# Sorting single columns of 104 edges with 128 places instead of double columns of 232 with 256, in a scatter-add kernel

## The chip, the cores and the metric

One core of a Trainium2 chip runs the whole program in one launch. The metric is the device time of one execution in microseconds (us); smaller is better. The engines are TensorE (PE; its weight loads are PEld), VectorE (DVE), ScalarE (ACT), GpSimd (POOL) and SyncE (SP, which here only issues transfers).

## The reference

There are 6250 nodes of 128 features and 206,250 edges of 128 features, fp32. The features of the edges are summed by the node in `src`; then a small network and a layer norm run over the nodes.

```python
x, src, dst, edge_attr_128          # (6250, 128), (206250,), (206250,), (206250, 128)
edge_aggr = jnp.zeros((n, 128)).at[src].add(edge_attr_128)
global_expand = jnp.repeat(global_feat, n, axis=0)
combined = jnp.concatenate([x, edge_aggr, global_expand], axis=-1) @ W_c + b_c
h = jax.nn.softplus(combined @ W1 + b1)
h = jax.nn.softplus(h @ W2 + b2)
out = layernorm(x + (h @ W3 + b3))
```

`src` is in no useful order. `dst` is not used by the result.

## The kernel before

**The sum over edges.** The nodes are cut into `NB` = 25 blocks of `BL` = 256. The kernel brings the edges of one block together in DRAM and then sums them with TensorE: 128 sorted edges (a chunk) are the stationary operand, and a one-hot block of 128 x 256, which says for each edge which of the 256 nodes it belongs to, is the moving one. The product is added into `sums_t`, which holds the sums of all nodes, features on partitions.

**Groups.** `GROUPS` cuts the edges into ten groups, given as (pairs, columns, sub). A group's edges are scattered into one of `PLACES` = 3 DRAM buffers (`place0` to `place2`), and while the next group is scattered, it is read back in chunks and reduced. A run of `sub` x 128 rows of a buffer holds edges of one block alone; rows that no edge fills keep what `fill_rows` wrote, or rows of an older group, whose node codes differ by `code_of(g)` and match nothing.

**Two ways into the buffer.** A plain column is 128 edges, one to a partition, that one indirect transfer writes row by row (516 bytes each: 128 features and the node code) to positions from `pos_of`. A pair is first sorted on chip. It is 232 edges, 120 on the partitions of one half and 112 of the other (`PA`, `PB`), which are put into 256 places by block so that each block's run begins at an even place. Two neighbouring places then go out as one run of 1032 bytes, so one indirect transfer of 128 runs takes the place of two of 128 rows.

**The sort.** `sort_steps(i)` handles one piece of five pairs. For each pair, `compare` makes the one-hot blocks `sort_hot` on ScalarE (two Abs of 256 columns, one Relu of 512), `gather` multiplies them with the edges on TensorE (four fp32 matmuls of 129 columns, two for each half of the places), and `settle` copies the result out of PSUM on ScalarE. The three are run for the next piece, within the loop's turn before its scatter.

**Positions.** `positions(g)` makes the list of steps that work out where each edge of a group goes. For pairs, the steps `count_set`, `count_set2`, `count_set3`, `place_set`, `rank_set` and `rank_set2` work on sets of `STEP` = 20 pairs, with pairs and blocks along the free dimension (500 elements), the same on all partitions. For plain columns they are `count`, `count2`, `scan`, `place` and `place2`; `totals` and `chunk_map` give the group's layout.

**The order.** TensorE, VectorE, ScalarE and SyncE run in the order in which the program issues their work. The main loop goes over groups and, in each, over pieces (ten plain columns or five pairs, mixed evenly). At each piece it loads the piece `LEAD` = 4 ahead, copies node codes in (`code_rows`), scatters the piece at hand, and then runs a share of four lists, merged evenly: the positions of the next group, the reduction of the last one (`reduce_steps`), the node rows, and the fill of the next group's buffer. `AHEAD` says by which part of the group a list is done.

**The reduction.** `reduce_steps(g)` reads `CHUNK_ROWS` = 1024 rows at a time (`load`), makes one-hot blocks of four chunks each (`match`: one VectorE instruction, or four Abs and a Relu on ScalarE), multiplies (`product`) and adds the result of each run of `sub` chunks to `sums_t` (`add`). `TAIL` says for the last four groups how loads are shared between VectorE and ScalarE: with (100, 2, 5, 5) a load i of these groups goes to ScalarE unless i modulo the number is its highest remainder.

```python
GROUPS = ((0, 40, 1), (40, 40, 2), (80, 80, 4), (100, 110, 4), (100, 110, 4), (100, 110, 4),
          (60, 80, 4), (40, 40, 2), (0, 40, 1), (0, 20, 1))
```

After the last group the node network runs over 13 tiles of up to 512 nodes.

## Time and profile before

| | |
|---|---|
| median of 3 runs | 2342.2 us (2340.88 to 2345.74) |
| the profiled execution | 2346.94 us; its span, first to last instruction, 2345.2 us |
| busy: TensorE, its weight loads | 1878.4 us (80%), 1547.6 us (66%) |
| busy: VectorE, ScalarE, GpSimd | 1424.1 us (61%), 1371.8 us (58%), 1227.8 us (52%) |
| transfers | 471.68 MB, mean 201 GB/s |
| mean granted TensorE clock | 0.914 |

A row of a group reads: line, engine, operation, output and inputs, shapes and count; then busy time in us and the mean of one in ns; then the idle time of the engine just before these instructions, and what ended it. Mean times overlap where an engine starts an instruction before the last has ended; busy time counts each moment once. A row of a stretch of time reads: from and to, length, then for each engine its busy time and the number of instructions, the granted clock, the share of the 16 DMA engines, and what they moved. A row of transfers reads: what, who issues it, count, KB each, and the median time from issue to landing.

### The profile page before, as it was taken

How to read it: one execution, taken by the hardware profiler on the slowest of the kernel's cores; microseconds unless marked ns; L12 is line 12 of the kernel's file. 1: busy time of each engine (PE TensorE's matmuls, PEld its weight loads, DVE VectorE, ACT ScalarE, POOL GpSimd, SP SyncE). 2: the span in 40 equal slices, each digit the busy share in tenths (PEclk: the TensorE clock that was granted, in tenths of full speed). 3: DMA queues.
4: the chain of work that ended last, by engine and by line, in shares of the span. 5: the costliest groups of instructions: out<-in, count | busy, mean ns of one | idle time of the engine just before them, and what ended most of it. 6: DMA issues, size and time to landing. Idle time of an engine off the chain costs nothing.

```text
span 2345.2 us, 31352 instructions
## 1 busy us (share of the span) xinstructions
PE 1878.4 (80%) x9590; PEld 1547.6 (66%) x9590; DVE 1424.1 (61%) x2493; ACT 1371.8 (58%) x3024; POOL 1227.8 (52%) x1258
## 2 busy tenths in 40 slices
PE   2567668888899788999779888879998667767886
PEld 0446556777778677778567777769888555646753
DVE  8687558648785578875368768447775011115767
ACT  0535445765555565555355454454444899986976
POOL 4664655776666566556456545565546123362006
PEclk9878779989999999999889999989999799898998
DMA  9999899979989698778477766768776444345442
GB/s 274 282 293 284 230 282 269 265 199 278 262 234 257 168 251 226 192 208 216 125 208 190 180 173 179 186 187 227 204 216 171 134 113 133 115 129 163 131 141 73
DMA packets 433910, 471.68 MB, mean 201 GB/s; under 512 B 35788, under 2 KB 305060, under 8 KB 433742
## 3 DMA queue, kind: packets, MB, share of 16 engines
q1 hardware_dynamic: 387133, 359.77, 59.4%
q0 software_dynamic: 46464, 109.88, 14.8%
q8 instruction: 77, 1.26, 0.2%
q14 instruction: 92, 0.75, 0.1%
q10 hardware_dynamic: 144, 0.02, 0.0%
HBM read 272.49 MB, written 200.11 MB: 202 GB/s over the span
## 4 chain that ended last, share of the span: by engine, by line
PE 44%; DMA 19%; ACT 16%; DVE 6%; issue 6%; POOL 5%; SPq 3%; DVEq 0%; ACTq 0%; POOLq 0%
PE part L599 30%; PE sorted L789 11%; DMA place<-fill 6%; ACT hot L580 6%; DMA chunks<-place 4%; POOL place L826 4%; DMA place<-rows,pos 3%; ACT hot L582 3%; DMA rows<-in_edge_attr 3%; SPq L158 3%; ACT sort_hot L779 2%; ACT sort_hot L781 2%; POOL place L820 1%; DVE hot L585 1%; DMA place<-pairs,pair 1%
## 5 line engine op out<-in xcount | busy, mean ns | idle before, releaser
L599 PE MATMUL part<-hot,chunks 128*128 128x256 f32 x4726 | 1181.2, 407 | 259.7 <-DVE hot L585 135.7
L599 PEld LDWEIGHTS part<-hot,chunks 128*128 128x128 f32 x4726 | 943.8, 205 | 452.2 <-ACT hot L582 151.4
L820 POOL DMA_INDIRECT place<-pairs,pair x520 | 520.9, 1002 | 621.6 <-ACT pairs L793 466.9
L826 POOL DMA_INDIRECT place<-rows,pos x669 | 653.8, 977 | 361.2 <-issue 217.0
L585 DVE SCALAR_TENSOR_TENSOR hot<-chunks,iota_ps 128x1024 f32<-128x1024 f32 x472 | 558.9, 1214 | 206.0 <-DMA chunks<-place 125.6
L793 ACT COPY pairs<-sorted 128x258 f32<-128x258 f32 x520 | 188.0, 368 | 823.2 <-PE sorted L789 796.1
L789 PE MATMUL sorted<-rows,sort_hot 120*128 120x129 f32 (+1 forms) x4160 | 562.8, 289 | 104.4 <-ACT sort_hot L781 93.9
L789 PEld LDWEIGHTS sorted<-rows,sort_hot 120*128 120x128 f32 (+1 forms) x4160 | 540.4, 201 | 143.0 <-ACT sort_hot L781 110.4
L619 DVE TENSOR_TENSOR sums_t<-sums_t,part 128x256 f32 x803 | 335.9, 418 | 329.9 <-PE part L599 302.2
L779 ACT ACTIVATE sort_hot<-by_slot,slot 120x256 f32<-120x256 f32 x1040 | 467.9, 498 | 5.2 <-DVE slot L388 5.2
L781 ACT ACTIVATE sort_hot<-sort_hot,ones 120x512 f32<-120x512 f32 x520 | 375.3, 722 | 16.9
L580 ACT ACTIVATE hot<-iota_f,chunks 128x256 f32<-128x256 f32 x475 | 201.0, 494 | 37.9 <-DMA chunks<-place 24.8
L582 ACT ACTIVATE hot<-hot,ones 128x1024 f32<-128x1024 f32 (+1 forms) x119 | 136.4, 1146 | 3.9
L1043 POOL TENSOR_TENSOR x_sb<-x_sb,b_all 128x512 f32<-128x512 f32 (+1 forms) x13 | 15.3, 1212 | 114.5 <-PE y_ps L985 114.3
L757 ACT COPY rows<-pair_i 120x5 f32<-120x5 f32 x208 | 30.8, 199 | 42.1 <-DMA place<-rows,pos 21.0
L388 DVE TENSOR_REDUCE slot<-small 128x20 f32<-128x500 f32 x52 | 34.8, 673 | 32.9 <-PE small L384 32.9
L694 DVE COPY x_t<-small 128x512 f32<-128x512 f32 (+1 forms) x13 | 8.6, 659 | 60.5 <-PE small L692 60.5
L489 DVE TENSOR_TENSOR first<-small,ib 128x500 f32<-128x500 f32 (+2 forms) x35 | 22.8, 651 | 30.5 <-PE small L480 30.1
L352 DVE TENSOR_TENSOR set_start<-first,even 128x500 bf16<-128x500 f32 x26 | 17.7, 683 | 37.5 <-PE small L382 36.3
L491 DVE TENSOR_REDUCE pos<-first 128x20 int32<-128x500 f32 (+2 forms) x35 | 37.5, 1070 | 1.2
L500 DVE COPY end_t<-small 25x1 f32<-25x1 f32 x10 | 1.4, 144 | 59.6 <-PE small L499 59.6
L457 DVE TENSOR_TENSOR_SCAN so_far<-iota_ps,ib 128x1500 bf16<-128x1500 f32 (+4 forms) x15 | 37.0, 2469 | 0.0
(164 smaller groups left out, 869.3 us busy)
## 6 DMA issues: line engine op xcount, KB each, us to landing
chunks<-place SPq DMA_DIRECT2D x295, 516.0 KB, 4.9
place<-fill SPq DMA_DIRECT2D x306, 258.0 KB, 9.5
rows<-in_edge_attr SPq DMA_DIRECT2D x66, 640.0 KB, 8.9
rows<-in_edge_attr SPq DMA_DIRECT2D x104, 300.0 KB, 6.4
rows<-in_edge_attr SPq DMA_DIRECT2D x104, 280.0 KB, 7.5
place<-rows,pos POOLq DMA_INDIRECT x669, 6.4
place<-pairs,pair POOLq DMA_INDIRECT x520, 5.7
x_sb<-in_x SPq DMA_DIRECT2D x24, 256.0 KB, 5.4
```

The lines of the kernel that those rows point to most:

```text
L158: ins = engine.dma_start(out, in_).ins
L580: nc.scalar.activation(hot[:, j], codes, AF.Abs, bias=chunks[i][:, lo + j, D:W], scale=-1.0)
L582: nc.scalar.activation(hot[:, :m], hot[:, :m], AF.Relu, bias=ones[:, :1], scale=-1.0)
L585: nc.vector.scalar_tensor_tensor(hot[:, :m], chunks[i][:, lo:lo + m, D:W].to_broadcast([P, m, BL]), code_of(g), iota_ps.unsqueeze(1).to_br ...
L599: nc.tensor.matmul(part[:, s - q, :], t[:, s * sub + j, :D], hot_of[i, (s * sub + j) // HALF * HALF][:, (s * sub + j) % HALF], start=(j == ...
L619: nc.vector.tensor_add(here, here, part[:, s - q, :])
L779: nc.scalar.activation(hot[:PA, q], by_slot.rearrange("p a b -> p (a b)")[:PA], AF.Abs, bias=slot[:PA, q, t0 + j:t0 + j + 1], scale=-1.0)
L781: nc.scalar.activation(hot[:PA], hot[:PA], AF.Relu, bias=ones[:PA, :1], scale=-1.0)
L789: nc.tensor.matmul(out[:, half, :], hot[:n, q, half * P:(half + 1) * P], two[:n, q * PAIRS + j, :], start=(q == 0), stop=(q == 1))
L793: nc.scalar.copy(sets_at[i][:, j], sums_of.pop(j))
L820: s = nc.gpsimd.indirect_dma_start(out=dst, out_offset=bass.IndirectOffsetOnAxis(ap=at, axis=0), in_=rows[:, j].rearrange("p a b -> p (a b ...
L826: s = nc.gpsimd.indirect_dma_start(out=dst, out_offset=bass.IndirectOffsetOnAxis(ap=at, axis=0), in_=rows[:r, j, :], in_offset=None)
```

## The change

The pair now has two single columns of 104 edges (`PN`), and each column is sorted by itself into 128 places, of which 64 runs of two go out; the two columns share one indirect transfer of 128 runs. A piece is six plain columns or three pairs (`LOAD_COLS` = 6). There are 600 pairs instead of 520 and 637 plain columns instead of 669, in eight groups that all have `sub` = 2, and two places.

- Sort: a unit is up to three columns of one parity. `compare` makes three Abs of 128 columns and one Relu on ScalarE, `gather` three fp32 matmuls of 129 columns with 104 rows, `settle` two copies of 64 partitions. `sort_steps(i)` settles the piece two ahead of the one being scattered, gathers the one three ahead and compares the one four ahead (`COMPARED` = 4). Loads run `LEAD` = 8 pieces ahead, node codes `CODED` = 5.
- Positions of pairs: four columns and their 26 buckets stand on 104 partitions (`KB`), so that counts, running sums and jumps of a set of 20 columns are matmuls with tables of 104 x 104 and VectorE operations of a few elements. The places within a column no longer depend on the group's totals.
- `TAIL` gives one load in three of the last four groups to ScalarE.

The diff, cut to what carries it; "..." marks what is left out.

```diff
-GROUPS = ((0, 40, 1), (40, 40, 2), (80, 80, 4), (100, 110, 4), (100, 110, 4), (100, 110, 4),
-          (60, 80, 4), (40, 40, 2), (0, 40, 1), (0, 20, 1))
-LOAD_COLS = 10
-PA, PB = 120, 112
+GROUPS = ((0, 60, 2), (70, 50, 2), (90, 50, 2), (130, 60, 2), (140, 90, 2), (170, 80, 2),
+          (0, 160, 2), (0, 70, 2))
+LOAD_COLS = 6
+PN = 104
 STEP = 20
+QUAD = 4
+THREE = 3
-TAIL = (100, 2, 5, 5)
+TAIL = ((1, 3), (1, 3), (1, 3), (1, 3))
-PLACES = 3
+PLACES = 2
-LEAD = 4
+LEAD = 8
+CODED = 5
+COMPARED = 4
...
-        sets_p = phase.enter_context(tc.tile_pool(name="sets", bufs=4))
+        sets_p = phase.enter_context(tc.tile_pool(name="sets", bufs=5))
-        sort_p = phase.enter_context(tc.tile_pool(name="sort", bufs=4))
+        sort_p = phase.enter_context(tc.tile_pool(name="sort", bufs=5))
...
             def count_set(t):
+                ib = pairs_in.tile([PN, STEP, NB + 1], BF16, name="pair_ib")
                 in_set[t] = ib
+                cols = slice(2 * s0 + t, 2 * s0 + t + STEP)
                 nc.vector.tensor_tensor(
+                    ib, pair_block[:, cols].unsqueeze(2).to_broadcast([PN, STEP, NB + 1]),
+                    iota_ps[:PN, :NB + 1].unsqueeze(1).to_broadcast([PN, STEP, NB + 1]),
                     op=ALU.is_equal)
...
+                small = whole(ps.tile([P, 4, P], F32, name="small", bufs=2))
+                small_of[t] = small
+                for q in range(per_set):
+                    nc.tensor.matmul(
+                        small[:KB, 500 + q:501 + q],
+                        ib[:, q * QUAD:(q + 1) * QUAD].rearrange("p t b -> p (t b)"),
+                        ones_h[:PN, :1], start=True, stop=True)
+
+            def even_set(t):
+                q0 = t // QUAD
+                even_i = per.tile([KB, per_set], I32, name="even_i")
+                small = small_of[t]
+                nc.vector.tensor_scalar(even_i, small[:KB, 500:500 + per_set], 1.0, None,
+                                        op0=ALU.add)
+                nc.vector.tensor_scalar(even_i, even_i, 510, None, op0=ALU.bitwise_and)
+                nc.vector.tensor_copy(evens[:, q0:q0 + per_set], even_i)
+                nc.tensor.matmul(small[:KB, 506:506 + per_set], lower_h,
+                                 evens[:, q0:q0 + per_set], start=True, stop=True)
+
+            def rank_set(t):
+                q0 = t // QUAD
+                small = small_of[t]
+                nc.vector.tensor_copy(starts[:, q0:q0 + per_set], small[:KB, 506:506 + per_set])
+                spread = pairs_in.tile([KB, per_set, P], BF16, name="spread")[:, :, :KB]
+                nc.vector.tensor_tensor(
+                    spread, unit_h.unsqueeze(1).to_broadcast([KB, per_set, KB]),
+                    starts[:, q0:q0 + per_set].unsqueeze(2).to_broadcast([KB, per_set, KB]),
+                    op=ALU.mult)
+                pr = small[:PN, :STEP * NB]
+                nc.tensor.matmul(pr, rank_h, in_set.pop(t)[:, :, :NB], start=True, stop=False)
+                for q in range(per_set):
+                    nc.tensor.matmul(
+                        pr[:, q * QUAD * NB:(q + 1) * QUAD * NB], ones_h[:KB, :PN],
+                        spread[:, q].rearrange("k (t b) -> k t b", b=NB + 1)[:, :, :NB],
+                        start=False, stop=(q == per_set - 1))
+
+            def slot_set(t):
+                nc.vector.tensor_reduce(
+                    slot_of[g][:PN, t:t + STEP],
+                    small_of.pop(t)[:PN, :STEP * NB].rearrange("p (t b) -> p t b", b=NB),
+                    axis=mybir.AxisListType.X, op=ALU.max)
...
+            def pair_set(t):
+                q0 = t // QUAD
+                past = pairs_in.tile([KB, per_set, P], BF16, name="spread")
+                nc.vector.tensor_tensor(
+                    past, twice[:KB].unsqueeze(1).to_broadcast([KB, per_set, P]),
+                    starts[:, q0:q0 + per_set].unsqueeze(2).to_broadcast([KB, per_set, P]),
+                    op=ALU.is_ge)
+                small = whole(ps.tile([P, 4, P], F32, name="small", bufs=2))
+                small_of["pair", t] = small
+                for q in range(per_set):
+                    for h in range(2):
+                        nc.tensor.matmul(small[:, q * QUAD:(q + 1) * QUAD], past[:, q],
+                                         got["jump"][:, q0 + q, h], start=(h == 0), stop=(h == 1))
+
+            def pair_set2(t):
+                at = small_of.pop(("pair", t))[:, :STEP].rearrange("p (b two) -> p b two", two=2)
+                for n in range(2):
+                    rows = slice(64 * n, 64 * n + 64)
+                    nc.vector.tensor_scalar(pair_of[g][rows, t // 2:(t + STEP) // 2],
+                                            at[rows, :, n], half_p[rows], None, op0=ALU.add)
...
-            for n, t in enumerate(sets):
+            for t in sets:
+                if t:
+                    steps.append(lambda t=t: rank_set(t - STEP))
                 steps.append(lambda t=t: count_set(t))
-                steps.append(lambda t=t: count_set2(t))
-                if n:
-                    steps.append(lambda t=t: count_set3(t - STEP))
+                if t:
+                    steps.append(lambda t=t: slot_set(t - STEP))
+                steps.append(lambda t=t: even_set(t))
...
-                share = TAIL[g - G] if g >= G - len(TAIL) else 1
-                if i % share != share - 1:
+                by, of = TAIL[g - G] if g >= G - len(TAIL) else (0, 1)
+                if i % of < by:
...
-                for q, (e, n) in enumerate(((0, PA), (PA * TB, PB))):
-                    rows_dma(two[:n, q * PAIRS:q * PAIRS + k, :D],
-                             edge_attr[e:e + n * TB, :].rearrange("(p t) d -> p t d",
-                                                                  p=n)[:, c:c + k, :])
+                rows_dma(two[:PN, :2 * k, :D],
+                         edge_attr[:E0, :].rearrange("(p t) d -> p t d",
+                                                     p=PN)[:, 2 * c:2 * (c + k), :])
...
+        def compare(unit):
+            i, lo, m, n = unit
+            g, _, c, _, _ = pieces[i]
             slot = slot_of[g]
+            hot = sort_p.tile([P, THREE, P], F32, name="sort_hot")
+            hot_of[unit] = hot
+            for j in range(m):
+                at = 2 * (c - groups[g][4] + lo + j) + n
+                nc.scalar.activation(hot[:PN, j], by_slot[:PN], AF.Abs,
+                                     bias=slot[:PN, at:at + 1], scale=-1.0)
+            nc.scalar.activation(hot[:PN, :m], hot[:PN, :m], AF.Relu, bias=ones[:PN, :1],
+                                 scale=-1.0)
+
+        def gather(unit):
+            i, lo, m, n = unit
+            hot = hot_of.pop(unit)
+            out = ps.tile([P, THREE, W], F32, name="sorted", bufs=2)
+            sorted_of[unit] = out
+            for j in range(m):
+                nc.tensor.matmul(out[:, j, :], hot[:PN, j],
+                                 rows_at[i][:PN, 2 * (lo + j) + n, :], start=True, stop=True)
+
+        def settle(unit):
+            i, lo, m, n = unit
+            if i not in sets_at:
+                sets_at[i] = sets_p.tile([P, PAIRS, 2, W], F32, name="pairs")
+            out = sorted_of.pop(unit)
+            for h in range(2):
+                nc.scalar.copy(sets_at[i][64 * n:64 * n + 64, lo:lo + m, h, :],
+                               out[64 * h:64 * h + 64, :m, :])
+
+        def sort_steps(i):
+            first, second, third = (units(i + COMPARED - k) for k in range(3))
             steps = []
+            for u in range(max(len(first), len(second), len(third))):
+                def one(u=u):
+                    if u < len(third):
+                        settle(third[u])
+                    if u < len(second):
+                        gather(second[u])
+                    if u < len(first):
+                        compare(first[u])
                 steps.append(one)
             return steps
...
                     load_rows(i + LEAD)
-                    code_rows(i + LEAD - 1, True)
+                    code_rows(i + CODED, True)
                     code_rows(i, False)
                     scatter_rows(i)
+                    now = [sort_steps(i)]
                     i += 1
...
-                    now.append(sort_steps(i))
```

Left out are the steps `all_sets` to `goals3`, run once a group, which turn the counts of all sets into the group's totals and into the jump from each bucket's place to its position, the function `tables`, which makes the constant tables once on VectorE, and the sizes of tiles that follow from the new shapes.

More of the change, by code (lines that the diff above doesn't have):

```diff
@@ L221, in whole_nodes @@
         def whole_nodes(part, n):
[L222 to L225 removed]
+            node = scratch("first")[:part.shape[0], :n]
+            wrap = scratch("second")[:part.shape[0], :n]
             nc.vector.tensor_copy(node, part)
@@ new lines, in all_sets3, with goals @@
+            def all_sets3():
+                got["all"] = per.tile([P, NB], F32, name="all")
+                nc.vector.tensor_copy(got["all"], small_of.pop("all")[:, 256:256 + NB])
+            def goals():
+                small = whole(ps.tile([P, 4, P], F32, name="small", bufs=2))
+                small_of["goals"] = small
+                goal = per.tile([1, QUAD, NB + 1], F32, name="goal")
+                nc.vector.tensor_copy(goal[:, :, :NB],
+                                      got["next"][:1].unsqueeze(1).to_broadcast([1, QUAD, NB]))
+                nc.vector.memset(goal[:, :, NB:], FAR)
+                nc.tensor.matmul(small[:KB, :1], goal.rearrange("p t b -> p (t b)"),
+                                 ones[:1, :1], start=True, stop=True)
@@ new lines, in goals2 @@
+            def goals2():
+                small = small_of["goals"]
+                base = per.tile([KB, 1], F32, name="base")
+                nc.vector.tensor_copy(base, small[:KB, :1])
+                nc.vector.scalar_tensor_tensor(
+                    earlier[:, :quads], earlier[:, :quads], base, starts[:, :quads],
+                    op0=ALU.add, op1=ALU.subtract)
+                nc.tensor.matmul(small[:KB, 128:128 + quads], minus, earlier[:, :quads],
+                                 start=True, stop=True)
@@ L519, in positions @@
                 if k == 0 and sets:
-                    steps.append(lambda: count_set3(sets[-1]))
+                    steps.append(all_sets3)
                 if k:
@@ L761, in code_rows, with units @@
             copy(rows_at[i][:r, :k, D:W], low[:r, c:c + k].unsqueeze(2))
[L763 removed]
+        def units(i):
             if i >= len(pieces) or pieces[i][1] != "pair":
                 return []
[L767 to L803 removed]
@@ L858 @@
             node_codes(0)
-            for i in range(LEAD - 1):
+            for i in range(CODED):
                 code_rows(i, True)
```

302 lines of the change are left out of this document (142 added, 160 removed).

## The prediction

> **What bounds the kernel now.** I cut the span where GpSimd's count of scatters (the x of POOL) reaches the end of each group (40, 80, 160, 210, 210, 210, 140, 80, 40, 19) and read the busy times stage by stage; the page's shares mix stages with different limits.
>
> ```profile
> core 0: us, PE busy (x) PEld busy (x) DVE busy (x) ACT busy (x) POOL busy (x), PEclk, DMA share, GB/s
> 0.00:30.10 30.10, 5.55 (x13) 1.29 (x13) 23.67 (x74) 1.79 (x5) 6.83 (x9) 1.00 0.92 268
> 30.10:90.90 60.80, 30.57 (x119) 16.68 (x119) 52.88 (x106) 21.30 (x54) 41.01 (x41) 0.96 1.04 276
> 90.90:234.10 143.20, 97.15 (x461) 74.46 (x461) 101.39 (x196) 66.64 (x159) 81.27 (x81) 0.78 1.07 289
> 234.10:483.30 249.20, 191.62 (x1004) 157.41 (x1004) 161.23 (x272) 141.08 (x331) 159.57 (x160) 0.85 0.94 258
> 812.40:1169.80 357.40, 309.08 (x1702) 263.93 (x1702) 245.72 (x366) 190.61 (x451) 207.33 (x211) 0.95 0.75 203
> 1169.80:1545.80 376.00, 323.01 (x1720) 274.30 (x1719) 255.64 (x407) 190.81 (x451) 207.39 (x210) 0.92 0.70 183
> 1545.80:1789.70 243.90, 232.62 (x1284) 207.99 (x1283) 168.82 (x237) 115.38 (x271) 136.17 (x141) 0.98 0.79 215
> 1789.70:2035.40 245.70, 172.64 (x776) 138.71 (x774) 36.02 (x93) 214.86 (x427) 78.56 (x86) 0.87 0.44 123
> 2035.40:2104.20 68.80, 46.61 (x213) 35.86 (x211) 9.00 (x23) 64.76 (x124) 39.32 (x44) 0.95 0.46 135
> ```
>
> Three regimes: until 483 us the DMA engines are full (share 0.92 to 1.07, about 280 GB/s). From 812 to 1790 us TensorE sets the pace, busy 0.865 of the first of these stages (309.08 of 357.40 us), 0.859 of the second, 0.954 of the third. From 1790 us it is ScalarE (0.874, then 0.94), with VectorE busy for 36 of 246 us: TAIL gives ScalarE all one-hot blocks of group 6.
>
> Next, the groups of the stage from 812.4 to 1169.8 us, for prices and for what TensorE waits on.
>
> ```profile
> L599 PE MATMUL part<-hot,chunks 128*128 128x256 f32 x810 | 194.7, 396 | 18.2 <-DVE hot L585 18.2
> L789 PE MATMUL sorted<-rows,sort_hot 112*128 112x129 f32 (+1 forms) x790 | 103.9, 283 | 20.6 <-ACT sort_hot L781 18.9 <-ACT pairs L793 1.7
> L585 DVE SCALAR_TENSOR_TENSOR hot<-chunks,iota_ps 128x1024 f32<-128x1024 f32 x102 | 120.7, 1214 | 30.9 <-PE part L599 16.4 <-DMA chunks<-place 14.4
> ```
>
> An fp32 matmul is two records. A chunk (128 sorted edges) costs 2 x 194.7/810 = 0.48 us, a sort record 103.9/790 = 0.1315 us. Of the 48 us in which TensorE is idle, 18.2 wait for VectorE and 18.9 for ScalarE's sort blocks.
>
> **The new work.** Chunks follow from the code's formula: two times (rows + 25 x 255) // 256, where a group's rows are 128 x columns + 256 x pairs. For the eight groups that is 108, 238, 278, 368, 418, 468, 208 and 136, together 2222 (2363 before). Stage n scatters group n, reduces group n-1, prepares group n+1. There are 600 + 637 scatters (520 + 669 before).
>
> **TensorE, sort.** A pair falls from eight records to four: 0.526 us instead of 1.052. Over all: 2400 x 0.1315 = 316 us against 4160 x 0.1315 = 547.
>
> **TensorE, positions.** A set of 20 columns (60 sets, each of 10 pairs, replace 26 of 20 pairs) now issues one matmul of 500 columns and 21 short ones, of 1, 4, 5 or 100 columns, each with its own weight load. No short bf16 matmul stands in the trace. The nearest rows:
>
> ```profile
> L379 PE MATMUL small<-pair_ib,before_h 128*128 128x500 bf16 x52 | 21.1, 406 | 10.9 <-DVE slot L388 10.9
> L379 PEld LDWEIGHTS <-before_h 128*128 128x128 bf16 x52 | 5.3, 102 | 0.7 <-issue 0.3
> L658 PE MATMUL small<-cols,wc_sb 128*128 128x1 f32 x2 | 0.3, 209 | 0.0
> L475 PE MATMUL small<-ib,upto_h 128*128 128x500 bf16 (+2 forms) x35 | 14.1, 403 | 0.0
> L692 PE MATMUL small<-ident,x_sb 128*128 128x128 f32 (+1 forms) x49 | 8.7, 304 | 16.7 <-DMA x_sb<-in_x 16.6
> L700 PE MATMUL small<-x_t,fold 128*128 128x512 f32 (+1 forms) x26 | 13.6, 608 | 0.0
> ```
>
> From below, the load alone: 0.10 us. From above, load and the whole record of a one-column matmul, 0.102 + 0.209 = 0.31. I take 0.13, near the lower end, since records overlap (the sort's mean is 283 ns, its share 131). A set is 21 x 0.13 + 0.41 = 3.1, with something for the 100 columns 3.2 us (2.5 to 6.9). Row positions stay: five passes of 0.40 us for 20 columns. So do the node rows, 22.3 us over three stages.
>
> **ScalarE.** A unit of three columns costs three Abs of 128, a Relu of 384 and two copies of 387 elements.
>
> ```profile
> L779 ACT ACTIVATE sort_hot<-by_slot,slot 120x256 f32<-120x256 f32 x1040 | 467.9, 498 | 5.2 <-DVE slot L388 5.2
> L781 ACT ACTIVATE sort_hot<-sort_hot,ones 120x512 f32<-120x512 f32 x520 | 375.3, 722 | 16.9
> L582 ACT ACTIVATE hot<-hot,ones 128x1024 f32<-128x1024 f32 (+1 forms) x119 | 136.4, 1146 | 3.9
> L580 ACT ACTIVATE hot<-iota_f,chunks 128x256 f32<-128x256 f32 x475 | 201.0, 494 | 37.9 <-DMA chunks<-place 24.8
> L793 ACT COPY pairs<-sorted 128x258 f32<-128x258 f32 x520 | 188.0, 368 | 823.2 <-PE sorted L789 796.1
> ```
>
> From 512 to 1024 columns the time rises by 424 ns, 0.83 ns a column. So an Abs of 128 lasts 498 - 106 = 392 ns. Two in a row overlap by 96 (467.9/1040 = 450 against 498), which leaves 392 + 2 x 296 = 984 for three. The Relu takes 722 - 106 = 616, a copy 368 + 107 = 475, and copies that overlap as the Abs do 430. A unit is 2.46 us (2.74 with no overlap at all), so a pair costs 1.64 us, and before 450 x 2 + 722 + 368 = 1.99, for more edges. Per edge that is a draw. TAIL's new (1, 3) for the last four groups gives every third load of eight chunks to ScalarE: 8 x 0.423 + 2 x 1.146 = 5.68 us.
>
> [...]
>
> **VectorE.** Per load of eight chunks: two matches and four additions, 2 x 1.214 + 4 x 0.418 = 4.1 us (two additions before in the groups of sub 4).
>
> ```profile
> L619 DVE TENSOR_TENSOR sums_t<-sums_t,part 128x256 f32 x803 | 335.9, 418 | 329.9 <-PE part L599 302.2
> L388 DVE TENSOR_REDUCE slot<-small 128x20 f32<-128x500 f32 x52 | 34.8, 673 | 32.9 <-PE small L384 32.9
> L369 DVE SCALAR_TENSOR_TENSOR first<-set_start,two_p,first 128x520 f32<-128x520 bf16 x26 | 19.7, 759 | 0.9
> L341 DVE TENSOR_TENSOR all<-all,all_more 128x25 f32<-128x25 f32 x19 | 3.5, 186 | 0.7
> L360 DVE TENSOR_TENSOR_SCAN second<-by_block,first 128x500 f32<-128x500 f32 x26 | 31.2, 1199 | 0.9
> ```
>
> A set has four operations of 500 to 640 elements (about 0.7 to 0.8 us by L388 and L369) and six of a few elements (0.19 by L341): 4.1 us. Stage 4: 46 loads x 4.1 + 17 sets x 4.1 + some 25 for rows and nodes = 283 us, below TensorE's 321: no bound. What goes is place_set, a step with a dozen operations up to 1.2 us long (L360) in a row; TensorE's 18.2 us of waiting for hot blocks stands behind such steps. What comes is a short exchange between TensorE and VectorE at each step of a set, with TensorE's own matmul queued behind VectorE's answer. The sort blocks, made four pieces ahead, no longer make TensorE wait (18.9). I let these cancel and keep the share 0.865.
>
> **DMA.** Fills go from 306 to 222 (80.8 to 58.5 MB) as two places replace three.
>
> ```profile
> chunks<-place SPq DMA_DIRECT2D x295, 516.0 KB, 4.9
> place<-fill SPq DMA_DIRECT2D x306, 258.0 KB, 9.5
> place<-rows,pos POOLq DMA_INDIRECT x669, 6.4
> L826 POOL DMA_INDIRECT place<-rows,pos x669 | 653.8, 977 | 361.2 <-issue 217.0 <-DMA rows<-in_edge_attr 68.9 <-DMA cols<-in_L_gnn_b 22.6
> L619 DVE TENSOR_TENSOR sums_t<-sums_t,part x803: 399/420/443, 106.1 to 2269.2; 128x256 f32 x161
> ```
>
> The first scatter waits until SyncE's queue has passed group 0's fill: 7.1 MB of it, eight loads (3.1) and the indices (0.8) are 11.1 MB, at 268 GB/s 41 us (30 before). Queued behind on SyncE, the later loads start later by the same. With two places, group n+2's scatters stand on GpSimd behind the reads of group n, which SyncE issues by 0.95 of stage n+1: nothing, or one landing of 4.9 us at each of six seams. Of the moved sort steps, the Abs and copies stand on ScalarE behind the codes of piece i+5, whose load was issued three pieces before (i+8): in the DMA-bound stages that queue still halts on loads, for POOL and TensorE both, and I count it in those stages' bytes.
>
> [...]
>
> **The sum, by stage.** Stage 0 (60 scatters): 41 us, then 23.1 MB (15.7 of fill for group 1) at 280 GB/s: 84; together 125. Stage 1: loads 10.7, fill 11.2, scatters 11.7 (a pair scatter writes some 116 of its 128 runs of 1032 bytes: 104 edges a column and, of 25 buckets, half padded by one), reads 7.1 = 40.7 MB, 146 and a little at the seam, 148; TensorE 122. Stage 2: TensorE 90 x 0.526 + 238 x 0.48 + 13 x 3.2 + 6 for row positions = 209, over 0.865 = 242 (DMA: 51.3 MB, 183). Stage 3: 130 x 0.526 + 278 x 0.48 + 14 x 3.2 + 17 = 264, over 0.865 = 305 (DMA: 65.0 MB, 232). Stage 4: 140 x 0.526 + 368 x 0.48 + 17 x 3.2 + 16 = 321, giving 371 (74.4 MB). Stage 5: ScalarE now binds: 114 units x 2.46 + 18 loads x 5.68 + 14 for codes = 396, at 0.94 421 (TensorE 324, giving 375). Stage 6: TensorE 468 x 0.48 = 225, at 0.954 236 (52 MB; GpSimd 160 x 1.30, from 977 ns and 217/669 of issue, 208). Stage 7: GpSimd 87 x 1.30 = 113, 115 with the seam. End: landing 6.4 and read 4.9, 136 x 0.48 = 65, then as before from the last addition to the end, 2345.2 - 2269.2 - 0.4 = 75.6: 152. Together 2115 us of span. The profiled execution took 2346.94, 1.7 more than its span, and stands 4.7 above the median 2342.2; so 2115 + 2 - 5 = 2112 us.
>
> Where that comes from: before, 1546 us bring in the first 160,160 edges and 799 the other 46,090 and the end; now 1612 bring in 174,720 and 503 the other 31,530 and the end. The front stages run at 9.2 ns an edge instead of 9.7 and take in 14,560 edges more, and the ScalarE-bound stretch behind them goes.
>
> **Rivals.** (1) The look-ahead removes the waits and the short steps add none: TensorE at 0.95 from stage 2 to 4. (209 + 264 + 321)/0.95 = 836 instead of 918: 2030 us. For it: the 0.954 of the stage from 1545.8 us, with fewer sorts and positions. Against: 60 sets with four exchanges each. Chance 0.17.
> (2) ScalarE's short instructions do not overlap and it is at 0.874, as in its own stage: stage 5 becomes (114 x 2.74 + 116)/0.874 = 490, 69 more: 2181 us. Chance 0.15.
> (3) Slower: the position steps stall TensorE. At the upper price a set costs 6.9 us, and four hand-overs of about half a microsecond (between L341 and L388) add 2: 8.9 instead of 3.2, over the 53 sets of stages 1 to 4 and 0.865. Stage 1 first has to use up its slack of 7 us, so 5.7 x 53/0.865 - 7 = 342: 2454 us. It turns the sign from 230 us on, which is about 7.1 us a set. Against: TensorE's queue holds gathers and products between the steps. Chance 0.11.
> (4) The change does not do what it says: the saved matmuls lie beside transfers. With reads in runs of 1032 bytes the rate falls to 200 GB/s: stages 0 to 6 then 157, 204, 256, 325, 372, 421, 260, with the rest 2262 of span, 2259 us. Against: 289 GB/s in a stage that read such runs or shorter. Chance 0.05.
> (5) Gains and stalls cancel: 0.02.
>
> My forecast has 0.50. The measurement tells about 0.2% (5 us) from no change. The range 2010 to 2290 holds the forecast, rivals 1, 2 and 4, and short matmuls up to some 0.27 us each; it leaves out rival 3. Faster 0.87, same 0.02, slower 0.11.
>
> **What would show it.** Right: L870's records 2400 at about 0.13 us; the last scatter near 1965 us; ScalarE busy above 0.9 in the stage with 250 scatters; VectorE above 150 us in the stage with 160 scatters. Wrong: idle time of TensorE put down to starts, spread or jump in stages 2 to 4 above 60 us a stage (rival 3); DMA share above 0.9 past 600 us (rival 4); position sets above 7 us.

## The result and the profile after

The changed kernel takes 2079.24 us (median, 2076.73 to 2080.52) against 2342.9 beside it: ratio 0.8873, 95% interval 0.8857 to 0.8888, so 11.3% faster. Forecast were 2112 us, 9.8% less, with a range of 2010 to 2290. The times are to be compared by ratio: the kernel before took 2342.9 us here, and 2325 to 2327 beside all experiments but the last. Single stages differ more: in two traces with the same instructions in it, stage 4 took 364.70 and 381.10 us, so a difference of that size in one of stages 2 to 4 shows nothing by itself.

The stretches of the changed kernel, cut as before at the counts of scatters (60, 120, 140, 190, 230, 250, 160, 87); the first row ends at the first scatter, the last one begins after the last:

```profile
core 0: us, PE busy (x) PEld busy (x) DVE busy (x) ACT busy (x) POOL busy (x), PEclk, DMA share, GB/s
0.00:37.80 37.80, 7.82 (x18) 1.82 (x18) 28.93 (x101) 2.35 (x11) 6.92 (x9) 1.00 0.97 304
37.80:129.50 91.70, 41.44 (x257) 28.87 (x257) 54.31 (x151) 27.36 (x74) 58.63 (x60) 1.00 1.01 256
129.50:286.60 157.10, 120.66 (x655) 99.03 (x655) 101.97 (x214) 100.82 (x265) 119.40 (x121) 0.84 0.98 256
286.60:514.20 227.60, 193.40 (x1149) 158.66 (x1149) 186.93 (x369) 154.38 (x401) 138.73 (x141) 0.92 0.83 229
514.20:818.30 304.10, 248.43 (x1442) 208.28 (x1443) 214.40 (x409) 219.81 (x569) 189.11 (x190) 0.89 0.78 217
818.30:1183.00 364.70, 299.86 (x1706) 247.38 (x1705) 274.96 (x522) 234.95 (x611) 226.96 (x231) 0.90 0.78 210
1183.00:1607.10 424.10, 336.20 (x1619) 275.91 (x1618) 226.17 (x392) 385.95 (x911) 246.17 (x267) 0.88 0.71 187
1607.10:1811.80 204.70, 176.62 (x801) 154.53 (x802) 153.54 (x263) 98.55 (x178) 158.82 (x187) 0.90 0.85 236
1811.80:1922.70 110.90, 105.48 (x478) 91.35 (x478) 92.75 (x158) 57.20 (x103) 86.25 (x101) 0.98 0.89 239
1922.70:2078.70 156.00, 130.89 (x547) 98.52 (x545) 121.21 (x318) 93.58 (x162) 44.10 (x51) 0.92 0.46 131
```

Stage by stage, forecast and measured: 125 and 129.5 us (stage 0, with the start), 148 and 157, 242 and 228, 305 and 304, 371 and 365, 421 and 424, 236 and 205, 115 and 111, end 152 and 156. Three readings matter. In stages 2 to 4 no engine is full: TensorE is busy for 0.85, 0.82 and 0.82 of the time, VectorE for 0.82, 0.71 and 0.75. In stage 5 ScalarE nearly is (385.95 of 424.10, 0.91). In stage 6 GpSimd issues its 160 scatters back to back, 204.70/160 = 1.28 us each: the record of a plain column's scatter lasts 0.961 us (mean of the 150 there), and 112 times the trace puts idle time ahead of one down to "issue", 34.1 us or 0.30 each.

The groups that carry the terms of the sum:

```profile
L680 PE MATMUL part<-hot,chunks 128*128 128x256 f32 x4444 | 1108.7, 408 | 153.7 <-DVE hot L666 91.7 <-ACT hot L663 61.7
L870 PE MATMUL sorted<-rows,sort_hot 104*128 104x129 f32 x2400 | 384.1, 305 | 101.2 <-ACT pairs L879 61.6 <-DMA rows<-in_edge_attr 23.4 <-ACT sort_hot L861 15.6
L368 PE MATMUL small<-spread,ones_h 104*104 104x100 bf16 x300 | 27.5, 231 | 9.2 <-DVE spread L361 9.0
L339 PE MATMUL small<-ones_h,pair_ib 104*104 104x1 bf16 x300 | 26.6, 200 | 13.8 <-DVE pair_ib L332 13.5
L366 PE MATMUL small<-pair_ib,rank_h 104*104 104x500 bf16 x60 | 26.4, 440 | 8.8 <-DVE starts L359 8.8
L453 PE MATMUL small<-jump,spread 104*128 104x4 bf16 x600 | 23.6, 165 | 12.1 <-DVE spread L445 12.1
L353 PE MATMUL small<-evens,lower_h 104*104 104x5 bf16 x60 | 10.5, 175 | 7.4 <-DVE evens L352 7.4
L859 ACT ACTIVATE sort_hot<-by_slot,slot 104x128 f32<-104x128 f32 x1200 | 393.3, 391 | 3.7
L861 ACT ACTIVATE sort_hot<-sort_hot,ones 104x384 f32<-104x384 f32 x404 | 247.1, 612 | 13.1
L879 ACT COPY pairs<-sorted 64x387 f32<-64x387 f32 (+2 forms) x808 | 384.0, 475 | 395.2 <-PE sorted L870 304.6 <-PE small L353 68.2 <-DMA place<-pairs,pair 12.9
```

For comparison, the sort's matmuls in the kernel before:

```profile
L789 PE MATMUL sorted<-rows,sort_hot 120*128 120x129 f32 (+1 forms) x4160 | 562.8, 289 | 104.4 <-ACT sort_hot L781 93.9
```

They fell from 562.8 us of busy time to 384.1, and their wait for sort blocks from 93.9 to 15.6 us. All idle time ahead of them, however, is nearly what it was, 101.2 us for 104.4: 61.6 us of waiting for the copies out of PSUM and 23.4 for the loads came in its place. A position set takes TensorE (27.5 + 26.6 + 26.4 + 23.6 + 10.5)/60 = 1.9 us. ScalarE's Abs of 128 takes 393.3/1200 = 328 ns, the forecast 984/3; the copies take their full 384.0/808 = 475 ns.

### The profile page after: what moved, and what is told of

Same layout as the page of the kernel before. It is cut to its first block, busy times and chain, and to the rows that moved or that the text cites. A ratio compares the mean times of both kernels' runs of the same rounds, so it can differ in the third digit from the quotient of the medians.

```text
span 2078.7 us, 30773 instructions
## 1 busy us (share of the span) xinstructions
PE 1660.8 (80%) x8663; PEld 1364.3 (66%) x8663; DVE 1455.2 (70%) x2892; ACT 1374.9 (66%) x3282; POOL 1275.1 (61%) x1352
## 4 chain that ended last, share of the span: by engine, by line
PE 37%; DMA 21%; issue 11%; ACT 11%; DVE 10%; POOL 8%; SPq 2%; DVEq 0%; POOLq 0%; ACTq 0%
PE part L680 30%; DMA place<-fill 6%; DMA place<-rows,pos 5%; DMA place<-pairs,pair 5%; POOL place L910 5%; PE sorted L870 4%; DVE hot L666 3%; ACT pairs L879 3%; POOL place L916 3%; ACT sort_hot L859 2%; DMA rows<-in_edge_attr 2%; DMA chunks<-place 2%; SPq L166 2%; ACT hot L661 2%; DVE sums_t L700 1%
## 5 line engine op out<-in xcount | busy, mean ns | idle before, releaser
L680 PE MATMUL part<-hot,chunks 128*128 128x256 f32 x4444 | 1108.7, 408 | 153.7 <-DVE hot L666 91.7
L680 PEld LDWEIGHTS part<-hot,chunks 128*128 128x128 f32 x4444 | 887.4, 205 | 333.9 <-DVE hot L666 108.9
L910 POOL DMA_INDIRECT place<-pairs,pair x600 | 596.8, 995 | 433.3 <-ACT pairs L879 239.6
L879 ACT COPY pairs<-sorted 64x387 f32<-64x387 f32 (+2 forms) x808 | 384.0, 475 | 395.2 <-PE sorted L870 304.6
L700 DVE TENSOR_TENSOR sums_t<-sums_t,part 128x256 f32 x1111 | 465.3, 419 | 186.5 <-PE part L680 144.6
L870 PE MATMUL sorted<-rows,sort_hot 104*128 104x129 f32 x2400 | 384.1, 305 | 101.2 <-ACT pairs L879 61.6
L870 PEld LDWEIGHTS sorted<-rows,sort_hot 104*128 104x128 f32 x2400 | 345.9, 212 | 134.9 <-ACT pairs L879 75.3
L859 ACT ACTIVATE sort_hot<-by_slot,slot 104x128 f32<-104x128 f32 x1200 | 393.3, 391 | 3.7
L861 ACT ACTIVATE sort_hot<-sort_hot,ones 104x384 f32<-104x384 f32 x404 | 247.1, 612 | 13.1
L663 ACT ACTIVATE hot<-hot,ones 128x1024 f32<-128x1024 f32 x106 | 121.7, 1148 | 3.5
L359 DVE COPY starts<-small 104x5 f32<-104x5 f32 x60 | 9.7, 162 | 86.2 <-PE small L353 86.2
L374 DVE TENSOR_REDUCE slot<-small 104x20 f32<-104x500 f32 x60 | 40.5, 674 | 23.4 <-PE small L368 22.6
L368 PEld LDWEIGHTS <-ones_h 104*104 104x104 bf16 x300 | 27.3, 145 | 33.8 <-issue 32.3
L361 DVE TENSOR_TENSOR spread<-unit_h,starts 104x520 bf16<-104x520 bf16 x60 | 42.0, 700 | 2.0
## 6 DMA issues: line engine op xcount, KB each, us to landing
rows<-in_edge_attr SPq DMA_DIRECT2D x104, 384.0 KB
```

What stands on the lines that cost most here:

```text
L663: nc.scalar.activation(hot[:, :m], hot[:, :m], AF.Relu, bias=ones[:, :1], scale=-1.0)
L680: nc.tensor.matmul(part[:, s - q, :], t[:, s * sub + j, :D], hot_of[i, (s * sub + j) // HALF * HALF][:, (s * sub + j) % HALF], start=(j == ...
L700: nc.vector.tensor_add(here, here, part[:, s - q, :])
L859: nc.scalar.activation(hot[:PN, j], by_slot[:PN], AF.Abs, bias=slot[:PN, at:at + 1], scale=-1.0)
L861: nc.scalar.activation(hot[:PN, :m], hot[:PN, :m], AF.Relu, bias=ones[:PN, :1], scale=-1.0)
L870: nc.tensor.matmul(out[:, j, :], hot[:PN, j], rows_at[i][:PN, 2 * (lo + j) + n, :], start=True, stop=True)
```

## The experiments

**The sharing rule alone, on the kernel before.**

```diff
-TAIL = (100, 2, 5, 5)
+TAIL = ((1, 3), (1, 3), (1, 3), (1, 3))
...
-                share = TAIL[g - G] if g >= G - len(TAIL) else 1
-                if i % share != share - 1:
+                by, of = TAIL[g - G] if g >= G - len(TAIL) else (0, 1)
+                if i % of < by:
```

> The kernel before with the changed kernel's rule of sharing alone (one load in three of the last four groups on ScalarE, the rest on VectorE). Theory (ScalarE set the pace from 1790 us): the stage of 245.7 us falls to what TensorE needs, 172.6 us of busy time over 0.95, about 185 us, and some 15 us go behind it; 2342 falls by 60 to 90 us, to 2250 to 2280. Rival (ScalarE was only waiting there too, for transfers or for TensorE): within 10 us of 2342.

Measured: 2264.6 us against 2325.26, ratio 0.9722 (0.9693 to 0.9751): 61 us. The stage that took 245.7 us:

```profile
1780.60:1966.80 186.20, 154.94 (x788) 134.58 (x787) 78.66 (x129) 120.96 (x254) 78.59 (x85) 0.91 0.59 166
```

It is 186 us, with ScalarE busy for 121 of them instead of 215. That ScalarE set the pace there is shown. On the kernel before, the rule alone is worth 2.8%, against 11.3 for the whole change.

**Two places alone, on the kernel before** (`PLACES = 3` to `2`).

> The kernel before with two places instead of three, and nothing else: fills fall from 80.8 to 53.9 MB, by 4 MB in the stage that fills for group 2, 7 for group 3, 11 for group 4, 5 for group 5. Theory (transfers bind until 483 us, TensorE behind that): 11 MB at 280 GB/s count, 40 us, and of the other 16 MB little; 30 to 60 us faster. Rival A (transfers bind wherever their share is 0.75 or more): all 27 MB, 96 us. Rival B (the reuse of a place makes GpSimd wait at the seams): no gain, or up to 30 us slower.

Measured: ratio 0.9899 (0.9872 to 0.9925), 21 to 22 us, below the theory's 30 and far below rival A's 96. Its stages 1 to 3, and then stages 1 and 2 of the run above, which has three places and was measured in the same session:

```profile
87.00:213.40 126.40, 86.18 (x402) 65.03 (x403) 95.36 (x177) 54.44 (x128) 80.80 (x80) 0.81 1.04 296
213.40:453.20 239.80, 190.87 (x1066) 159.03 (x1064) 169.71 (x295) 154.80 (x366) 160.22 (x161) 0.90 0.84 238
453.20:778.00 324.80, 282.10 (x1551) 240.27 (x1552) 212.88 (x315) 187.04 (x443) 206.58 (x210) 0.93 0.77 206
87.10:224.90 137.80, 97.12 (x438) 73.44 (x439) 101.46 (x196) 63.45 (x149) 80.63 (x80) 0.77 1.04 304
224.90:473.20 248.30, 194.64 (x1029) 159.94 (x1028) 162.73 (x274) 146.00 (x345) 159.04 (x160) 0.86 0.90 258
```

The stage with a share of 1.04 takes 126.40 instead of 137.80 us (8%; it took 143.20 in the trace of before, from another session). The next takes 239.80 instead of 248.30: 7 MB less (248.30 us at 258 GB/s against 239.80 at 238), which at 280 GB/s would be 25 us, bought 9. So transfers bound the first of them, and the second only in part; its share fell from 0.90 to 0.84.

**Both on the kernel before.**

> The kernel before with both the new sharing rule and two places: if the two gains (0.972 and 0.990) are in different stages they add, ratio 0.960 to 0.966; what is left to 0.887 then belongs to the sort, its look-ahead, the positions and the groups.

Measured: 0.9638 (0.96 to 0.9676). They add. So of the 11.3% these two lines give 3.6 on the kernel before, and 7.7 are left for the sort, its look-ahead, the positions and the groups. On the changed kernel the same lines can be worth something else: there two places instead of three are worth 0.7 points, not 1.0, as the next run shows.

**The changed kernel with three places** (`PLACES = 2` to `3`).

> The changed kernel with three places: fills rise from 58.5 to 82.8 MB, by 7 MB in stage 1, 9 in stage 2, 3 in stage 3, 6 in stage 4. If transfers bind only in stages 0 and 1: 25 us slower (ratio 0.898). If they bind through stage 4: 24 MB at 280 GB/s, 87 us (ratio 0.925). If the seam's wait for a place's reads cost anything with two places, less than 25.

Measured: 0.8944 (0.8905 to 0.8982), 0.7% or 17 us slower than the changed kernel. Stage 1 took 169.60 us in this trace instead of 157.10, stage 2 233.70 instead of 227.60.

```profile
119.60:289.20 169.60, 122.76 (x649) 101.09 (x649) 101.20 (x212) 98.28 (x257) 118.99 (x121) 0.81 1.01 282
289.20:522.90 233.70, 197.30 (x1154) 162.09 (x1154) 187.82 (x373) 156.85 (x409) 138.18 (x140) 0.91 0.90 257
```

Of the two theories the first holds, with 17 us for its 25: transfers bind in stage 1 and little behind it.

**Each matmul of the sort twice.**

```diff
             for j in range(m):
-                nc.tensor.matmul(out[:, j, :], hot[:PN, j], ...)
+                for _ in range(2):
+                    nc.tensor.matmul(out[:, j, :], hot[:PN, j], ...)
```

> The changed kernel with each matmul of the sort issued twice, so that a pair costs TensorE eight records again. Theory (TensorE sets the pace in stages 2 to 4 and the halved sort is worth its busy time there): 2400 records more at 0.13 to 0.16 us, over 0.85 in stages 1 to 5, less what hides beside ScalarE in stage 5: 260 to 380 us slower. Rival (transfers, ScalarE or GpSimd hide most of the sort): under 150 us slower.

Measured: 2122.57 us, ratio 0.9118 (0.9093 to 0.9143), 57 to 59 us slower than the changed kernel. The theory falls; the rival holds. The groups and three stages of this run:

```profile
L680 PE MATMUL part<-hot,chunks 128*128 128x256 f32 x4444 | 1051.5, 393 | 90.5 <-ACT hot L663 47.3 <-DVE hot L666 42.7
L871 PE MATMUL sorted<-rows,sort_hot 104*128 104x129 f32 x4800 | 640.3, 289 | 40.7 <-ACT pairs L881 27.0 <-ACT sort_hot L861 10.6 <-DMA rows<-in_edge_attr 2.8
514.70:834.60 319.90, 284.10 (x1950) 250.83 (x1951) 216.56 (x416) 219.99 (x570) 188.14 (x191) 0.96 0.75 206
834.60:1217.80 383.20, 340.18 (x2253) 296.82 (x2253) 274.77 (x522) 234.24 (x610) 227.56 (x231) 0.95 0.74 200
1217.80:1650.90 433.10, 384.25 (x2291) 334.33 (x2289) 225.89 (x393) 383.68 (x906) 246.15 (x266) 0.96 0.68 182
```

The sort's busy time grew by 256 us, but the reduction's, with the same 4444 records, fell by 57 as the granted clock rose (mean 0.903 to 0.951; 0.89 to 0.96 in stage 3, 0.90 to 0.95 in stage 4), and TensorE's idle time ahead of both groups fell from 254.9 (153.7 and 101.2) to 131.2 us (90.5 and 40.7). TensorE's share went up to 0.89 in each of the three stages. So TensorE had room in stages 2 to 4, and its busy time is no fixed amount of work. The run gives TensorE its old amount of sorting back, but not the old copies, positions or waits.

**The 600 matmuls of four columns twice** (line 453, the loop over `q` run twice).

> The changed kernel with the 600 matmuls of four columns (line 453) issued twice: 600 more short matmuls with their weight loads. Theory (after the profile: a short matmul takes 0.04 us, 23.6 us for 600): 15 to 30 us slower. The price of the prediction, 0.13 us: 60 to 90 us slower. The upper price, 0.31 us: about 190 us slower.

Measured: 0.8863 (0.8836 to 0.8891), no difference from 0.8873.

```profile
L453 PE MATMUL small<-jump,spread 104*128 104x4 bf16 x1200 | 38.7, 165 | 9.3 <-DVE spread L445 9.1
```

Another 15 us of busy time vanish in TensorE's gaps. None of the three prices stands: such a matmul took 23.6/600 = 39 ns of TensorE in the changed kernel, and 600 more of them cost the kernel nothing.

**The sort without look-ahead, on the changed kernel.**

```diff
         def sort_steps(i):
-            first, second, third = (units(i + COMPARED - k) for k in range(3))
+            mine = units(i)
...
+                    if u < len(mine):
+                        compare(mine[u])
+                    if 0 < u <= len(mine):
+                        gather(mine[u - 1])
+                    if u > 1:
+                        settle(mine[u - 2])
...
-                    now = [sort_steps(i)]
                     i += 1
+                    now = [sort_steps(i)]
```

> The changed kernel with the sort run as before, for the next piece alone within one turn (compare, gather one step on, settle two steps on), loads still eight ahead; ratio to the kernel before, where the changed kernel has 0.887. Theory 1 (the prediction: look-ahead is worth TensorE's wait for sort blocks, some 19 us in each of stages 2 to 5): 60 to 100 us slower than the changed kernel, ratio 0.91 to 0.93. Theory 2 (stages 2 to 4 are bound by queues that wait for each other and no engine is full, as the small cost of doubled sort matmuls suggests; the look-ahead is the main thing that went right): 120 us slower or more, ratio above 0.938. Rival: look-ahead is worth nothing beside the halved work, ratio 0.88 to 0.895.

Measured: 2464.19 us, ratio 1.0593 (1.0554 to 1.0633): slower than the kernel before, and 19% slower than the changed kernel. Its sort matmuls; two of its waits, the second followed by the same wait in the changed kernel; and its stage 4. A row of waits reads: engine, tile and line, what ended the wait; then us in total, how often, and the longest.

```profile
L870 PE MATMUL sorted<-rows,sort_hot 104*128 104x129 f32 x2400 | 433.6, 328 | 397.2 <-ACT sort_hot L861 397.0
POOL place L910 <- ACT pairs L879: 421.0, 92, 16.4
DVE sums_t L700 <- PE part L680: 303.7, 147, 13.7
DVE sums_t L700 <- PE part L680: 144.6, 115, 12.6
968.60:1413.70 445.10, 331.55 (x1718) 274.22 (x1717) 275.40 (x523) 238.16 (x621) 227.01 (x232) 0.83 0.63 173
```

TensorE waits 397.0 us for sort blocks instead of 15.6, and everything queued behind those matmuls waits with it: VectorE's additions 303.7 us instead of 144.6. All the work is the same, and stage 4 takes 445.10 us instead of 364.70. Theory 2 of this run is the one that its time fits, so the new sort is worth having only with its look-ahead. The likely reason, which no run isolates, is that a piece of two units has nothing to hide ScalarE's chain behind.

**Sort blocks one piece ahead, on the kernel before.** `compare` runs for the piece after next where that is in the same group; `gather` and `settle` stay; six buffers of `sort_hot` instead of four.

> [...] Theory (the look-ahead was the decisive part): TensorE's wait for sort blocks, 93.9 us in the trace of before, goes, 60 to 110 us faster, ratio 0.953 to 0.975. Rival (before had five pairs a piece to hide that wait behind, and the next wait, for copies, ends last): under 25 us, ratio above 0.989.

Measured: 0.9862 (0.9837 to 0.9887), 32 us, between the two.

```profile
L792 PE MATMUL sorted<-rows,sort_hot 120*128 120x129 f32 (+1 forms) x4160 | 555.2, 287 | 59.5 <-ACT pairs L797 37.1 <-ACT sort_hot L780 22.1
```

The wait for sort blocks went from 93.9 to 22.1 us; 37.1 of waiting for the copies out of PSUM came in its place. So this much of the look-ahead is worth 32 us on the kernel before. That its five pairs a piece had hidden the rest already is argued, not shown: `gather` and `settle` were not moved there.

**VectorE's reduction in `slot_set` twice.**

> The changed kernel with the reduction of slot_set issued twice: 60 x 0.67 = 40 us more of VectorE, nothing else. If VectorE's queue is what stages 1 to 4 wait on (the doubled sort cost 59 us for 256 us of TensorE): 30 us slower or more, ratio 0.900 or above. If it has room, as its 71 to 82 per cent suggest: under 12 us, ratio up to 0.893.

Measured: 0.8988 (0.8966 to 0.9011), 27 us slower for 40 us of added work (81.2 us instead of 40.5):

```profile
L376 DVE TENSOR_REDUCE slot<-small 104x20 f32<-104x500 f32 x120 | 81.2, 677 | 27.9 <-PE small L368 24.9
```

The expectation of a VectorE that is waited for set 30 us and more, the other under 12; it is near the first. A microsecond added to VectorE shows for two thirds (27 of 40), one added to the sort on TensorE for a quarter (59 of 256).

**Group 4's reduction on VectorE alone** (`TAIL` for the last three groups).

> The changed kernel with the reduction of group 4, which runs in stage 5, on VectorE alone (sharing for the last three groups only): ScalarE loses 102 us of work in stage 5, VectorE gains 44. Theory (ScalarE binds stage 5): that stage falls from 424 to what TensorE needs, 336/0.865 = 388, so 25 to 45 us faster, ratio 0.868 to 0.877. Rival (VectorE's additions and matches in one queue become the pace, as in the stages before): no gain or slower.

Measured: 2005.88 us, ratio 0.8613 (0.8577 to 0.865), 2.6 points better than the changed kernel and the best of the runs. Its stages 4 and 5:

```profile
803.00:1184.10 381.10, 309.81 (x1730) 255.67 (x1729) 277.31 (x527) 239.68 (x624) 226.94 (x231) 0.88 0.75 204
1184.10:1537.10 353.00, 307.28 (x1595) 258.19 (x1594) 261.77 (x423) 283.29 (x732) 244.76 (x254) 0.93 0.82 221
```

Stage 5 falls from 424.10 to 353.00 us with ScalarE at 283.29: it was bound by ScalarE. The fall is larger than the theory said; TensorE's busy time falls too (336.20 to 307.28), with a clock of 0.93 instead of 0.88. Stage 4, in which nothing was changed, took 16 us more in this trace than in that of the changed kernel (381.10 and 364.70).

**That, and one-hot blocks of the reduction one load ahead.**

```diff
-                    if i + 2 < n:
-                        load(i + 2)
-                    for lo in range(0, loads[i][1] * sub, HALF):
-                        match(i, lo)
+                    if i + 3 < n:
+                        load(i + 3)
+                    if i + 1 < n:
+                        matches(i + 1)
```

> The changed kernel with group 4's reduction on VectorE (ratio 0.861 by itself) and the one-hot blocks of the reduction made one load ahead (loads three ahead, five buffers of chunks). Theory (in stages 1 to 4 TensorE's products wait on VectorE's hot blocks through the order of the queues, 91.7 us in the trace of the changed kernel): 50 to 90 us faster than 0.861, ratio 0.82 to 0.84. Rival (VectorE's own work or the position steps' exchanges set the pace, and the order moves the wait elsewhere): ratio 0.855 to 0.87.

Measured: 0.8679 (0.8651 to 0.8707), no gain over 0.8613 but 0.7 points lost; the rival's range holds it. Its stages 2 and 3, and its end:

```profile
275.00:497.10 222.10, 185.75 (x1132) 153.52 (x1131) 186.18 (x365) 149.00 (x388) 139.81 (x140) 0.93 0.83 232
497.10:781.80 284.70, 239.24 (x1444) 201.06 (x1444) 216.05 (x414) 219.86 (x569) 188.96 (x191) 0.91 0.82 231
1834.30:2016.40 182.10, 148.97 (x614) 109.72 (x612) 136.59 (x339) 100.49 (x174) 43.98 (x50) 0.93 0.42 121
```

Stages 2 and 3 took 222 and 285 us against 227 and 300 in the run before it, no more than a stage differs by from trace to trace; the span behind the last scatters took 182 against 153. Why it did is not shown.

**The same for groups 0 to 3 alone.**

> The changed kernel with group 4's reduction on VectorE, and the one-hot blocks made one load ahead for groups 0 to 3 alone (their reductions run in stages 1 to 4; loads three ahead for all). In the run with look-ahead for all groups stages 2 and 3 were 5 and 15 us shorter than without it, the last two spans 40 us longer. Theory (the look-ahead helps where sorts and positions stand between the reductions and harms where ScalarE's and VectorE's blocks alternate): 20 to 45 us faster than 0.861, ratio 0.842 to 0.853. Rival (the gain in stages 2 and 3 was the scatter of runs, or the third load ahead does the harm): ratio 0.857 to 0.868.

Inconclusive. The kernel before took 2661.49 us beside it, not 2325, and this one 2493.65; TensorE waited 124.2 us in it for nothing that the trace shows, and the ratio of 0.9369 (0.9333 to 0.9405) can't be set beside the others. Whether it beats 0.8613 stays open.

```profile
PE part L680 <- issue: 124.2, 60, 18.2
```

## Why the prediction was right, and where it was right for the wrong reason

**Confirmed.** The kind of bound in stages 0 and 1 (transfers) and 5 (ScalarE), the ScalarE-bound tail before, and that the new rule ends it. VectorE was forecast at 283 us in stage 4 and took 274.96. The end was 156 us for 152.

The span came to 2078.7 us for 2115. Of the signs that the prediction named, two came (ScalarE above 0.9 in stage 5, VectorE at 153.54 us in stage 6) and two missed: a sort record took 0.160 us, not 0.13, and the last scatter came at 1922 us, not 1965.

**Terms mis-sized that cancel.** Two rows of stage 4 of the changed kernel (818.3 to 1183.0 us):

```profile
L680 PE MATMUL part<-hot,chunks 128*128 128x256 f32 x727 | 193.3, 421 | 33.4 <-DVE hot L666 33.4
L870 PE MATMUL sorted<-rows,sort_hot 104*128 104x129 f32 x548 | 84.3, 296 | 11.3 <-ACT pairs L879 9.0 <-ACT sort_hot L861 2.1
```

Over stages 2 to 4, the 44 position sets took 80 us of TensorE, 1.8 each, where 3.2 were put: 61 us too much. A sort record took 0.157 us (222.8/1415) instead of 0.1315, 33 us too little, and a chunk 0.524 us (two of the 1759 records, 461.3 us) instead of 0.48, 37 us too little. The clock was lower there (0.89 to 0.92, and 0.95 in the stage that gave the prices). For the sort the runs are also shorter, six records instead of eight; with twelve in a row (each matmul twice) a record took 640.3/4800 = 0.133 us at a clock of 0.951. No run separates the two.

**The step that failed though the sum held** is "over 0.865". It was wrong in two ways.

First, it divided one kind of sum by a share of another. The prices come from groups of instructions, which overlap each other on TensorE: in the stage from 812.4 to 1169.8 us the groups add up to 332.7 us, while TensorE was busy for 309.08, and 0.865 is the share of the latter. Measured over stages 2 to 4, the groups add up to 811 us (794 were forecast), TensorE was busy for 741.7 of 896.4 us, a share of 0.83. So 794 was 52 us too much as busy time and 0.865 was too high; that they gave 918 us, 2.4% from 896, is luck.

Second, TensorE's share was carried over from the kernel before as if it set the pace in stages 2 to 4. It didn't: doubling the sort there cost a quarter of its time, and 40 us on VectorE cost more than that in proportion. What fits all runs is a row of queues that wait for each other, each worked off in the order of the program, in which the sort, the positions and the reduction take turns. In the changed kernel's trace from 899.5 to 912 us, the steps of the sets come in that order on TensorE (L366, L368, L339, L353) and on VectorE (L361, L332, L374, L349), with waits of 0.87 us at L374 and 1.40 at L359 for TensorE. That such waits set the pace is argued, and no run shows it by itself. That the share came out near the forecast is no proof of the rule; the runs with more work on TensorE and on VectorE told the two apart.

**The second failed step** is the price of the moved sort. The forecast let look-ahead and hand-overs cancel, and rival 1 gave the two together 82 us. TensorE's wait for sort blocks did go, but waits for the copies and loads took its place. Undone alone, the look-ahead is worth about 400 us of this kernel. That much of it is a debt of the change itself, as smaller pieces need it, is argued; on the kernel before the part of it that was run is worth 32 us. How the remaining 7.7% divide between halved matmuls, positions and fewer, larger groups is not settled: undoing the halving on TensorE costs 2.5 points, and no run undid the positions or the groups.

**Stage 6** was forecast from TensorE at 236 us; it took 205, which is GpSimd's 160 x 1.28. The forecast had that bound at 208 as the lower one. TensorE's part was no bound, because the stage's reduction ran on into the next: 778 of its 936 records lie in stage 6. **Stage 1** took 157 us for 148: 256 GB/s, not 280. With three places the same stage moved 282 GB/s, so 256 is no cap on it; why it was 256 here is not shown.

**The rivals.** Rival 1 (TensorE at 0.95) did not occur, nor rival 3: position steps did make TensorE wait, but by 7 to 14 us for each kind over the whole kernel, 51 us for the five rows above; VectorE waited longer in the same exchanges, 86.2 us for TensorE at `starts`. Rival 2 was half right: the copies don't overlap (475 ns each), the Abs do (328 ns each for records of 391), and stage 5 ran at 0.91. Rival 4 did not occur as told: stages 2 and 3 moved 229 and 217 GB/s at shares of 0.83 and 0.78, so transfers did not set their pace. But most of the saved matmul time did lie beside other waits, as the doubled sort shows.

## What to carry to other kernels

A busy share that fits a forecast does not make the engine the bound: add work to it, and see whether the time moves by as much (here 57 to 59 us for 256). Run a pipeline across engines once without its look-ahead: here that took 2464.19 us instead of 2079.24; that smaller pieces need more of it is argued, not shown. And look for stages where one engine carries a job that its idle neighbour can share: two such lines, one on either kernel, gave 2.8 and 2.6 points.

## What the runs showed of the hardware

- TensorE's granted clock was highest in the one of three runs with the most work on TensorE: mean 0.903 in the changed kernel, 0.951 with the sort doubled and 0.839 without look-ahead, where TensorE waited 397.0 us for sort blocks instead of 15.6. A record of the same reduction took 1108.7/4444 = 0.249, 1051.5/4444 = 0.237 and 1189.0/4444 = 0.268 us: time times clock is 0.225, 0.225 and 0.224. So without look-ahead the records of the same work took 7% longer, beside the longer waits; why the clock was lower there no run isolates.
- A bf16 matmul of four columns with its own 128-column weight load took 23.6/600 = 39 ns of TensorE, two fifths of the 97 ns that the record of its load lasts; with each issued twice, 38.7/1200 = 32 ns.
- Consecutive Abs on ScalarE overlapped by some 95 ns in the changed kernel (1200 records of 391 ns took 393.3 us, in 404 units), the two copies from PSUM of a unit not at all (384.0/808 = 475 ns, the mean of one).
